# A first cross attention with scores by quarters of keys, transposed on VectorE, divided at the end on GpSimd

## The chip, the core and the metric

The kernel runs on one core of one Trainium2 chip. A core has a TensorE (matrix products, into the accumulator memory PSUM), a VectorE, a ScalarE (functions such as the exponential), a GpSimd and a SyncE that issues transfers; each works through its own queue in order, and they wait for each other through semaphores. PSUM has eight banks of 512 float32 words on each of 128 partitions. GpSimd does not appear in this kernel as a reader of PSUM. The metric is the device time of one execution in microseconds (us); less is better.

## The reference

The whole program is four layers of a perceiver, each a cross attention, a mixing block and a feed-forward block, with residual additions. The change is in the first cross attention alone. `x` is 16 batches of 64 query rows by 256, the context 16 batches of 1024 rows by 192; there are 16 heads of 16 columns:

```python
def _L0_xattn_ref(q_tokens, kv_tokens, Wq, Wk, Wv, Wo):
    q = q_tokens @ Wq.T
    k = kv_tokens @ Wk.T
    v = kv_tokens @ Wv.T
    ...
    attn = jnp.einsum('bhqd,bhkd->bhqk', q, k) * scale      # scale 1/4
    attn = jax.nn.softmax(attn, axis=-1)
    out = jnp.einsum('bhqk,bhkd->bhqd', attn, v)
    ...
    return out @ Wo.T

x = x + _L0_xattn_ref(_layernorm(x, axis=-1), ctx_768, ...)
```

## The kernel before, in words

`xattn_direct` (line 280) works batch by batch, and in each batch in four groups `c` of four heads, so in 64 steps `(b, c)`. Every operation on TensorE, VectorE (`dve`) and ScalarE (`act`) inside it goes through `in_order`, which ties each instruction to the one issued before it on the same engine: the order on these three engines is the order of the Python text. GpSimd's operations are not tied that way; the scheduler of the tile framework places them, in practice in the order of the text too.

A step of the loop at line 472 does work for three steps at once:

- `scores(*ahead)` (line 399): the scores of the next step, 4 heads by 64 queries by 1024 keys. The queries `qb` are stored so that a group of 32 partitions holds two heads, each multiplied by the mask of its own 16 rows (`own`), with zeros in the other's place. Two tiles `pss` of two banks each (e = 0, 1), 128 partitions (two heads by 64 queries) by 1024 keys, by four matmuls of 32 rows by 128 columns over 512 keys.
- `least` (line 408): VectorE's negated maximum of each tile. `exps` (line 413): ScalarE's exponential of a whole tile with that bias, and its sums by row. `shares` (line 419): VectorE's reciprocal of the sum and the multiplication of the exponentials.
- `transposes` (line 423): TensorE transposes of the exponentials in 128x128 blocks, 16 a step, into four PSUM banks in turn (`pst`), and a copy of each bank into `pT` by VectorE or ScalarE.
- `project` (line 356): a fourth of the key and value projections of the next batch (pieces 0, 1 keys; 2, 3 values), into two banks, copied out by VectorE and by ScalarE. Piece 0 issues the load of the next batch's transposed context on SyncE's queue.
- `values` (line 430): the products with the values for the step before, 32 matmuls of 128 rows by 32 columns over 64 queries, into a bank kept for all four groups (`both`). `keep` (line 442) copies it out once a batch.
- `queries(1, ...)` in steps 4 to 7 (second half of the query projections), `norm(1)` and `normed(1)` in steps 1 and 2, and `output` (line 447) once for two batches: product with `Wo` and the addition to `X`.

PSUM is divided into pools: `ps_s`, two tiles of two banks for the scores; `ps_t`, three banks for projections, transposes and the rest; `ps_o`, one bank for `both`. A tile of a pool is handed out in turn, and a writer waits until the readers of the tile's last use are done.

The second cross attention, `xattn_folded` (line 508), has forms that this change brings into the first one: scores by small column tiles, a stream transpose on VectorE, a matrix `same` that adds up quarters of the partitions. It is used below for durations.

Of the kernel before, what the change touches and what calls it, by code (L numbers as in the profile page):

```python
# [8 lines left out]
F32 = mybir.dt.float32  # L9
# [46 lines left out]
def bc(ap, axis, n):  # L56

    ap = ap.unsqueeze(axis)
    shape = list(ap.shape)
    shape[axis] = n  # L60
    return ap.to_broadcast(shape)
# [17 lines left out]
class Net:  # L79
# [113 lines left out]
    def copy(self, i, out, in_):  # L193

        if i % 2 == 0:
            self.nc.vector.tensor_copy(out, in_)
        else:
            self.nc.scalar.copy(out, in_)
# [81 lines left out]
    def xattn_direct(self, L):  # L280
# [6 lines left out]


        nc, tc, a = self.nc, self.tc, self.a
        dve, act = self.queue("dve", nc.vector), self.queue("act", nc.scalar)  # L290
# [5 lines left out]
        with ExitStack() as es:  # L296
            one = es.enter_context(tc.tile_pool(name=f"{L}one", bufs=1))
            two = es.enter_context(tc.tile_pool(name=f"{L}two", bufs=2))
            thr = es.enter_context(tc.tile_pool(name=f"{L}thr", bufs=2))
            ps_s = es.enter_context(tc.tile_pool(name=f"{L}ps_s", bufs=2, space=PSUM))  # L300
            ps_t = es.enter_context(tc.tile_pool(name=f"{L}ps_t", bufs=3, space=PSUM))
            ps_o = es.enter_context(tc.tile_pool(name=f"{L}ps_o", bufs=1, space=PSUM))

# [3 lines left out]
            )  # L307
            nc.vector.tensor_scalar(own, own, 0.25, None, ALU.mult)
            vs = [one.tile([P, NKC, H, 32], F32, name=f"v{i}") for i in range(2)]
            nc.gpsimd.memset(vs[0][:, :, :, 16:], 0.0)  # L310
# [41 lines left out]

            ctxs, kTs, os_ = {}, {}, {}
            both = ps_o.tile([P, 2, 4, TQ], F32, name="o")

            def project(b, piece):
# [6 lines left out]
                if piece < 2:  # L363
# [6 lines left out]
                    for i in range(2):  # L370
                        ms = slice((2 * piece + i) * 64, (2 * piece + i) * 64 + 64)
                        for n in range(2):
                            u, rows = (n ^ i) * 64, slice(n * 64, (n + 1) * 64)
                            self.mm(ps[i][u : u + 64, :], wk[rows, 1, ms], c1[rows, :], False, True)
                    for i, copy in enumerate((dve.tensor_copy, act.copy)):
                        copy(kTs[b][:, 2 * piece + i, :], ps[i])
                else:
# [7 lines left out]
                    for i in range(2):  # L385
                        for n in range(2):
# [7 lines left out]
                            )  # L394
                    for n, copy in enumerate((dve.tensor_copy, act.copy)):
                        j = 4 * n + 2 * jh
                        copy(v[:, j : j + 2, :, :16], ps[n].rearrange("p (i h d) -> p i h d", i=2, d=16))

            def scores(b, c):
                pss = [ps_s.tile([P, S], F32, tag="s", name="pss") for _ in range(2)]  # L400
                for n in range(2):
                    for e in range(2):
                        r = (n ^ (c % 2)) * 64 + e * 32
                        ql = qb[r : r + 32, c, b].rearrange("p h q -> p (h q)")
                        self.mm(pss[e][:, n * 512 : (n + 1) * 512], ql, kTs[b][r : r + 32, c, :])
                return pss

            def least(ps):
                nm = self.small.tile([P, 1], F32, tag="nm", name="nm", bufs=4)
                dve.tensor_reduce(nm, ps, AX.X, ALU.max, negate=True)  # L410
                return nm

            def exps(ps, nm):
                pr = thr.tile([P, S], F32, tag="pr", name="pr", bufs=4)
                sm = self.small.tile([P, 1], F32, tag="sm", name="sm", bufs=4)
                act.activation(pr, ps, AF.Exp, bias=nm, accum_out=sm)
                return pr, sm

            def shares(pr, sm):
                dve.reciprocal(sm, sm)  # L420
                dve.tensor_scalar(pr, pr, sm, None, ALU.mult)

            def transposes(dst, pr, jh, copy):
                pt = ps_t.tile([P, 512], F32, tag="t", name="pst")
                for j in range(4):
                    jj = jh * 4 + j
                    self.tr(pt[:, j * P : (j + 1) * P], pr[:, jj * P : (jj + 1) * P])
                copy(dst[:, jh * 4 : jh * 4 + 4, :], pt.rearrange("p (j q) -> p j q", q=P))

            def values(b, c, pT):  # L430
                o = both[:, b % 2]
                for j in range(NKC):
                    for h in range(4):
                        self.mm(
                            o[32 * h : 32 * h + 32, c, :],
                            vs[b % 2][:, j, 4 * c + h, :],
                            pT[:, j, h // 2, (h % 2) * TQ : (h % 2 + 1) * TQ],
                            j == 0,
                            j == NKC - 1,
                        )  # L440

            def keep(b):
                if b % 2 == 0:
                    os_[b // 2] = two.tile([P, 4, 2, TQ], F32, tag="oT", name="oT")
                act.copy(os_[b // 2][:, :, b % 2, :], both[:, b % 2])

# [12 lines left out]
            normed(0)  # L459
            project(0, 0)  # L460
            project(0, 1)
            for c in range(4):
                queries(0, c)
            steps = [(b, c) for b in range(B) for c in range(4)]
            pss = scores(0, 0)
            prs = [exps(pss[e], least(pss[e])) for e in range(2)]
            project(0, 2)
            project(0, 3)
            for p in prs:
                shares(*p)  # L470
            last = None
            for i, (b, c) in enumerate(steps):
                ahead = steps[i + 1] if i + 1 < len(steps) else None
                nxt, nms = [None, None], [None, None]
                if ahead:
                    pss = scores(*ahead)
                    nms = [least(ps) for ps in pss]
                pT = thr.tile([P, NKC, 2, P], F32, tag="pT", name="pT")
                transposes(pT[:, :, 0, :], prs[0][0], 0, act.copy)
                transposes(pT[:, :, 0, :], prs[0][0], 1, dve.tensor_copy)  # L480
                if ahead:
                    nxt = [exps(pss[e], nms[e]) for e in range(2)]
                    shares(*nxt[0])
                if b + 1 < B:
                    project(b + 1, c)
                if last:
                    values(*last)
                if ahead:
                    shares(*nxt[1])
                transposes(pT[:, :, 1, :], prs[1][0], 0, dve.tensor_copy)  # L490
                transposes(pT[:, :, 1, :], prs[1][0], 1, act.copy)
                if i == 1:
                    norm(1)
                if i == 2:
                    normed(1)
                if 4 <= i < 8:
                    queries(1, i - 4)
                if c == 0 and last:
                    keep(b - 1)
                if c == 1 and b % 2 == 0 and b > 0:  # L500
                    output(b // 2 - 1)
                prs, last = nxt, (b, c, pT)
            values(*last)
            keep(B - 1)
            output(NT - 1)
# [2172 lines left out]
```

## Time and profile before

| | us |
|---|---|
| median of three runs | 3171.4 (3170.1 to 3172.4) |
| the profiled execution | 3170.8 |
| its span, first to last instruction | 3168.8 |
| the stage of the change: first scores, and its last output product | 30.9 and 505.2 |

Mean granted TensorE clock of the profiled execution: 0.953; in the stage, from 58 to 500 us, it is 1.00. The engines' busy time in that stretch, whose length is 442.0 us:

| TensorE | VectorE | ScalarE | GpSimd |
|---|---|---|---|
| 436.2 | 371.8 | 251.8 | 9.1 |

A row of a group or of a timeline gives a line of the source (L72, L188, L191 are helpers through which all recorded operations pass), the engine (PE TensorE's matmuls, PEld its weight loads, DVE VectorE, ACT ScalarE, POOL GpSimd), the operation, the tiles it writes and reads (`out<-in`), its shape and a count. In a timeline the first two numbers are start and length; in brackets stands the idle time ahead and who ended it. A float32 matmul runs as two passes, so it counts twice. Matmuls of different row or column groups of the array overlap, so that the length of a group is not the sum of its parts. In the chain of waits, each piece starts where the one before it released it.

### The profile page before, as it was taken

How to read it: one execution, taken by the hardware profiler on the slowest of the kernel's cores; microseconds unless marked ns; L12 is line 12 of the kernel's file. 1: busy time of each engine (PE TensorE's matmuls, PEld its weight loads, DVE VectorE, ACT ScalarE, POOL GpSimd, SP SyncE). 2: the span in 40 equal slices, each digit the busy share in tenths (PEclk: the TensorE clock that was granted, in tenths of full speed). 3: DMA queues.
4: the chain of work that ended last, by engine and by line, in shares of the span. 5: the costliest groups of instructions: out<-in, count | busy, mean ns of one | idle time of the engine just before them, and what ended most of it. 6: DMA issues, size and time to landing. Idle time of an engine off the chain costs nothing.

```text
span 3168.8 us, 64106 instructions
## 1 busy us (share of the span) xinstructions
PE 2940.9 (93%) x26912; PEld 1772.9 (56%) x26912; DVE 1960.3 (62%) x4061; ACT 1348.4 (43%) x3035; POOL 712.7 (22%) x784
## 2 busy tenths in 40 slices
PE   7999999898899999979978999997999899998797
PEld 4666666665445544458854545434665455556676
DVE  6888886524666665971127676757884676765611
ACT  3555554312554541013324454438861255654211
POOL 1000002411110001014411000024771355541131
PEclk9999999999999999978988999998999999999889
DMA  2000000013223313017851222201111211210233
GB/s 74 32 32 32 28 22 15 14 37 105 61 78 92 98 45 82 21 65 270 294 162 53 70 71 73 59 21 39 41 54 37 64 57 63 70 44 14 94 108 122
DMA packets 73793, 223.00 MB, mean 70 GB/s; under 512 B 17457, under 2 KB 28580, under 8 KB 66594
## 3 DMA queue, kind: packets, MB, share of 16 engines
q1 hardware_dynamic: 45936, 113.99, 11.9%
q0 software_dynamic: 21840, 99.39, 9.4%
q10 hardware_dynamic: 5730, 5.53, 0.6%
q8 instruction: 212, 3.47, 0.5%
q14 instruction: 75, 0.61, 0.1%
HBM read 210.00 MB, written 12.66 MB: 70 GB/s over the span
## 4 chain that ended last, share of the span: by engine, by line
PE 79%; DVE 9%; issue 4%; ACT 4%; POOL 3%; DMA 1%; SPq 0%; ACTq 0%; POOLq 0%; DVEq 0%
PE pss L188 13%; PE o L188 12%; PE pu L188 6%; PE psp L188 5%; PE pkv L188 5%; PE pd L188 5%; PE py L188 4%; PE pst L191 4%; PE psc L188 3%; PE po L188 2%; DVE nm L72 2%; ACT pr L72 2%; PE pb L191 2%; PE psi L188 1%; PE psq L188 1%
## 5 line engine op out<-in xcount | busy, mean ns | idle before, releaser
L188 PE MATMUL pss<-cT,qw 128*32 128x256 f32 x8192 | 371.5, 387 | 23.0 <-ACT pr L72 23.0
L72 DVE TENSOR_REDUCE nm<-pss 128x2 f32<-128x512 f32 (+1 forms) x384 | 309.3, 861 | 86.3 <-PE pss L188 86.3
L188 PE MATMUL o<-pT,cx 128*64 128x512 f32 (+1 forms) x1024 | 355.4, 607 | 0.0
L72 ACT ACTIVATE pr<-pss,nmm 128x256 f32<-128x256 f32 x512 | 234.3, 483 | 164.8 <-DVE nmm L72 164.8
L188 PEld LDWEIGHTS pss<-cT,qw 128*32 128x32 f32 x8192 | 205.0, 110 | 173.0 <-ACT pr L72 33.1
L188 PEld LDWEIGHTS o<-pT,cx 128*64 128x64 f32 (+1 forms) x1024 | 127.8, 165 | 200.2 <-issue 187.8
L205 POOL TENSOR_SCALAR rs<-mv 128x8 f32<-128x8 f32 (+3 forms) x52 | 10.0, 193 | 877.1 <-DVE mv L221 444.4
L188 PE MATMUL pkv<-wx,cT 128*128 128x512 f32 (+1 forms) x512 | 193.3, 632 | 0.6 <-issue 0.6
L72 ACT ACTIVATE pr<-pr,sm 128x256 f32<-128x256 f32 x256 | 109.1, 497 | 184.2 <-DVE sm L72 184.2
L72 DVE TENSOR_SCALAR pr<-pr,sm 128x256 f32<-128x256 f32 (+1 forms) x384 | 170.6, 486 | 6.6
L72 DVE TENSOR_TENSOR_SCAN h<-dA,pb 128x512 f32<-128x512 f32 x128 | 154.5, 1217 | 15.8 <-PE pb L191 9.4
L1444 POOL TENSOR_TENSOR h<-h,cb 128x1024 f32<-128x1024 f32 x64 | 151.4, 2368 | 53.3 <-DVE h L72 51.0
L2304 DVE TENSOR_SCALAR y<-pd,row 128x256 f32<-128x256 f32 x39 | 18.9, 484 | 225.1 <-PE pd L188 175.7
L72 DVE STREAM_TRANSPOSE pT<-pr 128x1024 f32<-128x1024 f32 x128 | 151.8, 1224 | 2.2
L188 PE MATMUL pd<-wd,hT 128*128 128x256 f32 x656 | 149.3, 382 | 3.0 <-DVE hT L2492 1.4
L72 ACT ACTIVATE pr<-pss,nm 128x1024 f32<-128x1024 f32 x128 | 142.5, 1113 | 11.4 <-DVE nm L72 8.8
L191 PE MATMUL pst<-ident,pr 128*128 128x128 f32 x1024 | 140.6, 280 | 5.8 <-DVE sm L72 1.9
L72 ACT COPY pT<-pst 128x512 f32<-128x512 f32 x128 | 74.9, 585 | 163.8 <-PE pst L191 163.8
L191 PEld LDWEIGHTS pst<-ident,pr 128*128 128x128 f32 x1024 | 109.4, 141 | 61.5 <-ACT pT L72 26.5
L188 PEld LDWEIGHTS pd<-wd,hT 128*128 128x128 f32 x656 | 123.1, 190 | 31.4 <-DVE hT L2492 6.2
L1618 POOL TENSOR_TENSOR rnk<-rnk,mhalf 128x8 f32<-128x8 f32 (+1 forms) x84 | 130.0, 1548 | 7.0
L188 PE MATMUL py<-h,ident 128*128 128x512 f32 x256 | 130.7, 596 | 0.0
(525 smaller groups left out, 5700.2 us busy)
## 6 DMA issues: line engine op xcount, KB each, us to landing
cT<-in_ctxT SPq DMA_DIRECT2D x32, 768.0 KB, 4.4
cx<-in_ctxP SPq DMA_DIRECT2D x32, 768.0 KB, 4.3
cT<-in_ctxT SPq DMA_DIRECT2D x32, 512.0 KB, 4.3
cT<-in_ctxT SPq DMA_DIRECT2D x64, 256.0 KB, 6.1
offb<-d_off SPq DMA_DIRECT2D x16, 576.0 KB, 3.6
cb<-d_C SPq DMA_DIRECT2D x16, 512.0 KB, 3.8
wu<-in_L_ffn_w POOLq DMA_DIRECT2D x8, 1024.0 KB
wd<-in_L_ffn_w POOLq DMA_DIRECT2D x8, 1024.0 KB
```

What stands on the lines that cost most here:

```text
L72: ins = getattr(self.engine, op)(*args, **kwargs)
L188: self.in_order(self.nc.tensor.matmul(out, lhsT=lhsT, rhs=rhs, start=start, stop=stop))
L191: self.in_order(self.nc.tensor.transpose(out, in_, self.ident))
L205: nc.gpsimd.tensor_scalar(t[:p, :n], in_, scale, eps, ALU.mult, ALU.add)
L1444: nc.gpsimd.tensor_tensor(hs[i], hs[i], cbs[hf, g], ALU.mult)
L1618: nc.gpsimd.tensor_tensor(r, r, self.mhalf[:, : n * H], ALU.pow)
L2304: nc.vector.tensor_scalar(y[:, i, :], po[:, i * D : (i + 1) * D], weight[:, g + i : g + i + 1], None, ALU.mult)
```

## The change

It rewrites the step of the first cross attention:

- **PSUM.** `ps_s` has three tiles of two banks instead of two; `ps_t` two banks instead of three; `ps_o` goes. The output `o` of each step takes a bank of `ps_t`.
- **Scores** by quarters. The 128 partitions of a tile hold, for a group of 32, a quarter `qa` of the keys (every fourth run of 32 keys); the columns hold the halves of the keys `n`, the four quarters `q` of the query rows (two heads by two halves of 32 queries), and 128 keys. 64 matmuls of 32 rows by 32 columns over 128 keys take the place of four.
- **Maximum.** `largest` reduces a tile to four columns; GpSimd copies the four groups of partitions to one (`nw`), VectorE takes their minimum of the negated values (`least`), and GpSimd copies it to the other groups of partitions.
- **Exponentials** in four instructions a tile, a column of bias and of sums each.
- **Transposes.** `turn` is one VectorE stream transpose (32x32 blocks) per tile, straight into `pT`.
- **Division.** The exponentials are no longer multiplied. Once a batch `sums` adds the four groups' sums on TensorE, `inverse` takes the reciprocal and GpSimd spreads it over a masked matrix `rd`, `spread` turns that into a multiplier for each output on TensorE, and `keep` copies outputs and multiplier out and multiplies them on GpSimd.
- **Order.** The step transposes the first tile, then takes the maxima and the first tile's exponentials of the next step, then projections, values and `keep`, then the second tile's transpose and exponentials. `output` runs in the third group of a batch instead of the second.

```diff
-            ps_s = es.enter_context(tc.tile_pool(name=f"{L}ps_s", bufs=2, space=PSUM))
-            ps_t = es.enter_context(tc.tile_pool(name=f"{L}ps_t", bufs=3, space=PSUM))
-            ps_o = es.enter_context(tc.tile_pool(name=f"{L}ps_o", bufs=1, space=PSUM))
+            ps_s = es.enter_context(tc.tile_pool(name=f"{L}ps_s", bufs=3, space=PSUM))
+            ps_t = es.enter_context(tc.tile_pool(name=f"{L}ps_t", bufs=2, space=PSUM))
...
+            same = one.tile([P, 32], F32, name="same")
+            nc.vector.tensor_reduce(same, self.ident.rearrange("p (a x) -> p x a", x=32), AX.X, ALU.add)
+            fourth = one.tile([P, 32], F32, name="fourth")
+            nc.vector.memset(fourth, 0.25)
...
             def scores(b, c):
-                pss = [ps_s.tile([P, S], F32, tag="s", name="pss") for _ in range(2)]
-                for n in range(2):
-                    for e in range(2):
-                        r = (n ^ (c % 2)) * 64 + e * 32
-                        ql = qb[r : r + 32, c, b].rearrange("p h q -> p (h q)")
-                        self.mm(pss[e][:, n * 512 : (n + 1) * 512], ql, kTs[b][r : r + 32, c, :])
+                pss = [ps_s.tile([P, 2, 4, P], F32, tag="s", name="pss") for _ in range(2)]
+                kT = kTs[b][:, c].rearrange("p (k a y) -> p k a y", a=4, y=32)
+                for q in range(4):
+                    for n in range(2):
+                        for e in range(2):
+                            r = (n ^ (c % 2)) * 64 + e * 32
+                            for qa in range(4):
+                                self.mm(
+                                    pss[e][qa * 32 : (qa + 1) * 32, n, q, :],
+                                    qb[r : r + 32, c, b, q // 2, q % 2 * 32 : q % 2 * 32 + 32],
+                                    kT[r : r + 32, :, qa, :],
+                                )
                 return pss
...
+            def largest(ps):
+                nm = self.small.tile([P, 4], F32, tag="nm", name="nm", bufs=4)
+                dve.tensor_reduce(nm, ps.rearrange("p n q k -> p q n k"), AX.XY, ALU.max, negate=True)
+                w = self.small.tile([32, 4, 4], F32, tag="nw", name="nw", bufs=4)
+                for qa in range(4):
+                    nc.gpsimd.tensor_copy(w[:, qa], nm[qa * 32 : (qa + 1) * 32])
+                return w
+            def least(w):
+                m = self.small.tile([P, 4], F32, tag="nmm", name="nmm", bufs=4)
+                dve.tensor_reduce(m[:32], w.rearrange("p a q -> p q a"), AX.X, ALU.min)
+                nc.gpsimd.tensor_copy(m[32:64], m[:32])
+                nc.gpsimd.tensor_copy(m[64:], m[:64])
+                return m
+            def exps(b, c, e, ps, m):
+                if (c, e) == (0, 0):
+                    sms[b] = two.tile([P, 4, 2, 4], F32, tag="sm", name="sm")
+                pr = thr.tile([P, 4, 2, P], F32, tag="pr", name="pr", bufs=3)
+                for q in range(4):
+                    act.activation(
+                        pr[:, q], ps[:, :, q, :], AF.Exp, bias=m[:, q : q + 1], accum_out=sms[b][:, c, e, q : q + 1]
+                    )
+                return pr
+            def turn(b, c, e, pr):
+                if e == 0:
+                    pTs[b, c] = thr.tile([P, NKC, 2, 4, 32], F32, tag="pT", name="pT")
+                dve.transpose(
+                    pTs[b, c][:, :, e].rearrange("p k q x -> p q k x"),
+                    pr.rearrange("p q n (k y) -> p q (n k) y", y=32),
+                )
...
+            def sums(b, o):
+                ps = o[:, TQ : TQ + 32]
+                for qa in range(4):
+                    self.mm(ps[qa * 32 : (qa + 1) * 32], same, sms[b].rearrange("p c e q -> p (c e q)"))
+                return ps
+            def inverse(b, ps):
+                rc = two.tile([P, 32], F32, tag="rc", name="rc")
+                dve.reciprocal(rc, ps)
+                rds[b] = two.tile([P, 4, 2, 2, 2 * 32], F32, tag="rd", name="rd", bufs=1)
+                for c in range(4):
+                    nc.gpsimd.tensor_tensor(
+                        rds[b][:, c].rearrange("p e h (u x) -> p (e h u) x", x=32),
+                        bc(rc[:, 8 * c : 8 * c + 8], 2, 32),
+                        bc(same, 1, 8),
+                        ALU.mult,
+                    )
+            def spread(b, o):
+                for h in range(4):
+                    self.mm(o[32 * h : 32 * h + 32, P : P + 256], fourth, rds[b][:, :, h // 2, h % 2, :])
+            def keep(b, c, o):
+                if c == 0:
+                    oss[b] = two.tile([P, 4, TQ], F32, tag="os", name="os", bufs=1)
+                act.copy(oss[b][:, c], o[:, 0:TQ])
+                if c == 3:
+                    ra = two.tile([P, 4, TQ], F32, tag="ra", name="ra", bufs=1)
+                    act.copy(ra, o[:, P : P + 256].rearrange("p (c q) -> p c q", q=TQ))
+                    if b % 2 == 0:
+                        os_[b // 2] = two.tile([P, 4, 2, TQ], F32, tag="oT", name="oT")
+                    nc.gpsimd.tensor_tensor(os_[b // 2][:, :, b % 2, :], oss[b], ra, ALU.mult)
...
             for i, (b, c) in enumerate(steps):
                 ahead = steps[i + 1] if i + 1 < len(steps) else None
+                now = prs
                 if ahead:
                     pss = scores(*ahead)
+                turn(b, c, 0, now[0])
+                if ahead:
+                    ws = [largest(ps) for ps in pss]
+                    prs = [exps(*ahead, 0, pss[0], least(ws[0])), None]
                 if b + 1 < B:
-                    project(b + 1, c)
+                    projected(b + 1, c)
+                if last or c == 3:
+                    o = ps_t.tile([P, 512], F32, tag="t", name="o")
+                if c == 3:
+                    total = sums(b, o)
                 if last:
-                    values(*last)
+                    if last[1] == 3:
+                        spread(last[0], o)
+                    values(*last, o)
+                    keep(*last, o)
+                turn(b, c, 1, now[1])
                 if ahead:
-                    shares(*nxt[1])
+                    prs[1] = exps(*ahead, 1, pss[1], least(ws[1]))
+                if c == 3:
+                    inverse(b, total)
...
-                if c == 1 and b % 2 == 0 and b > 0:
+                if c == 2 and b % 2 == 0 and b > 0:
                     output(b // 2 - 1)
...
+            o = ps_t.tile([P, 512], F32, tag="t", name="o")
+            spread(B - 1, o)
+            values(*last, o)
+            keep(*last, o)
             output(NT - 1)
```

`projected` is `project` followed by its two copies, VectorE's of the first bank and ScalarE's of the second, as before.

## The prediction

> **What bounds the kernel now.** I read the page's slices first, then the chain that ended last, cut to steps of the first cross attention (about 31 to 505 us), then the timeline of the same steps. The change touches nothing else, so everything after 505 us only shifts. The chain (start, length, what) through one step:
>
> ```profile
> 153.79 1.03 PE o L188 x64
> 154.82 1.02 PE pst L191 x8
> 155.84 1.07 PE pss L188 x8
> 156.91 1.02 PE pst L191 x8
> 157.94 2.79 PE psp L188 x16
> 160.73 1.03 PE o L188 x64
> ```
>
> Every piece begins where the last one ends and all are TensorE: the step is 6.94 us (7.03 where keys are projected, psp then 2.89), and TensorE is its bound. VectorE is the next: from the groups of this stretch, with count, busy time, mean ns, and idle time ahead:
>
> ```profile
> L72 DVE TENSOR_REDUCE nm<-pss 128x1 f32<-128x1024 f32 x128 | 150.7, 1219 | 40.1 <-PE pss L188 40.1
> L72 DVE TENSOR_SCALAR pr<-pr,sm 128x1024 f32<-128x1024 f32 x128 | 96.7, 756 | 4.6
> L72 DVE COPY pT<-pst 128x512 f32<-128x512 f32 x128 | 87.7, 685 | 5.1 <-PE pst L191 1.2
> ```
>
> Per step that is two of each, about 5.3 us, and 0.69 for its share of the projections. So removing TensorE work alone can bring little over a microsecond a step, before VectorE binds.
>
> **TensorE's share.** Both pst pieces go: -2.04 us a step. The scores become 64 matmuls of 32x32 tiles over 128 columns, two passes each: 128 instructions in 8 rounds of 16 tiles. pst shows 128 columns in about 0.109 us (8 in 1.02, the rest being the change of tile shape). Do 16 tiles run side by side? The rows say so for 4 (o: 64 passes of 64 columns in 1.03 us) and, in the second attention, for 8:
>
> ```profile
> 905.90 1.96 PE L188 MATMUL pss<-cT,qw 64*32 64x256 f32 x64
> ```
>
> 64 passes of 256 columns, at 0.216 each if alone, take 1.96 us, 8 at a time. For 16 I take 8 x 0.109 and 0.17 for the first load and the change of shape: 1.05, as much as the 4 matmuls cost now. The upper end is 16.1 ns an instruction, o's 1.03/64: 128 x 16.1 = 2.06 us. A rule speaks against the change: the Trainium skill, "TensorE: Matmul & The Clock Gate", section "Wait — 56ns, not 53.3ns?", says that starts never lie closer than about 25 ns, however small the matmul. That would make 3.2 us, and take back the transposes. The rows contradict it: o's 64 in 1.03 us are already closer on average, so I don't use it. New on TensorE too: per batch `sums` (8 passes of 32 columns, 0.15) and `spread` (8 of 256, four at a time, 0.55), 0.2 a step. Sum: psp 2.84 + o 1.03 + 1.05 + 0.2 = 5.1 us.
>
> **The other engines' totals.** VectorE loses shares (2 x 0.94) and pT copies (2 x 0.68); it gains two stream transposes (2.37 for a pair below) and two small reductions (0.17, as nmm's copies of 32x8 take 0.165): 2.36 + 2.37 + 0.34 + 0.69 = 5.8. ScalarE: 8 exponentials at 0.45, 0.59 for the projection, 0.24 for `keep`: about 4.6. GpSimd: 12 small copies, and per step one 128x256 product of `inverse`: about 2.8. By totals the step would be 5.8 us. But the order decides, and it closes a loop.
>
> **The loop.** Of three score tiles, each step takes two, so the second tile of step s+1 is the first of step s. TensorE may write it only when the exponentials of step s's first tile are done. In ScalarE's order those come first; then, in every engine's order: scores(s+1) on TensorE, largest of both tiles on VectorE (after turn of step s), 4 + 4 copies on GpSimd, least, 2 copies on GpSimd, exponentials of s+1. The first tile's two copies stand in GpSimd's queue behind the second tile's four, so both reductions lie on the path. Rows for it, exponentials and transposes of the second attention:
>
> ```profile
> 900.35 0.47 ACT L72 ACTIVATE pr<-pss,nmm 128x256 f32<-128x256 f32 x1 [1.87 <-DVE nmm L72]
> 900.72 0.19 ACT L72 ACTIVATION_READ_ACCUMULATOR pr<-pss,nmm 128x1 f32 x1
> 900.81 0.47 ACT L72 ACTIVATE pr<-pss,nmm 128x256 f32<-128x256 f32 x1
> 901.46 2.37 DVE L72 STREAM_TRANSPOSE pT<-pr 128x1024 f32<-128x1024 f32 x2
> ```
>
> One exponential every 0.45; the fourth ends with its readout: 3 x 0.45 + 0.57 = 1.93. That scores wait for the readout is shown at the stage's end:
>
> ```profile
> 493.04 1.11 ACT L72 ACTIVATE pr<-pss,nm 128x1024 f32<-128x1024 f32 x1
> 494.05 0.19 ACT L72 ACTIVATION_READ_ACCUMULATOR pr<-pss,nm 128x1 f32 x1
> 494.30 0.31 PEld L188 LDWEIGHTS pss<-kT,qb 32*128 32x128 f32 x6 [0.84 <-ACT pr L72]
> ```
>
> The readout ends at 494.24, weights load at 494.30: 0.06. Small GpSimd copies the trace shows only as these:
>
> ```profile
> 504.86 0.23 POOL L789 COPY upto<-leq 64x64 f32<-64x64 f32 x1 [13.03 <-ACT pT L72]
> 505.04 0.23 POOL L790 COPY after<-gts 64x64 f32<-64x64 f32 x1
> 505.31 0.23 POOL L789 COPY upto<-leq 64x64 f32<-64x64 f32 x1
> 505.49 0.24 POOL L790 COPY after<-gts 64x64 f32<-64x64 f32 x1
> ```
>
> 64 elements: 0.23 long, 0.18 apart when independent; the dependent third starts 0.27 after. Fewer elements cost less (the 64x256 copies take 0.40, so 0.9 ns each): 4 elements would be 0.125 apart. Small tensor_scalars of 4 elements take 0.19. I take 0.15 apart and 0.185 long; ends 0.03 (one-element memsets of 0.1) and 0.25 (no overlap). Hand-overs: VectorE to GpSimd 0.08, GpSimd to ScalarE 0.05.
>
> Loop: 0.06 + scores 1.16 (1.05 and the last matmul's latency) + 0.05 + reductions 2.36 + 0.08 + four copies and the next start 0.60 + copy 0.185 + 0.08 + copy 0.185 + 0.05 + 1.93 = **6.75 us**, turn's 1.2 lying beside the scores. Against 6.98 a step the gain is 0.23, not 1.2: all four engines have slack, and what was hidden (the maximum's trip, the exponentials) binds. `inverse`'s four products (0.67 apart, from the 0.72 of 128x256 rows) run beside turn and largest, so cost nothing up to 0.9 each; at 1.3 they delay the copies and cost some 28 us in all.
>
> Costed at nothing: `keep` on ScalarE every step (0.24, ra 0.38 once a batch), hidden by about 2 us of slack there, at its own length otherwise; `same` and `fourth` at the start (about 0.3), beside the root of the first norm on GpSimd; the context's loads on SP, one per batch, 4.4 us to landing, unmoved. The weight loads that GpSimd issues for the next stage (0.8 each, three) now stand among the copies: 2 us at most, half of it slack, left out.
>
> **Extras now in the loop.** Transposes, projections and outputs share two banks instead of three, so psq and psy take the bank of psp's second half, whose ScalarE copy is queued behind the exponentials; and the next turn is queued on VectorE behind their result.
>
> ```profile
> 505.18 1.99 PE L188 MATMUL psy<-wo,oT 128*128 128x256 f32 x8 [0.47 <-ACT oT L72]
> 507.21 0.42 DVE L72 TENSOR_TENSOR X<-X,psy 128x256 f32<-128x256 f32 x1 [3.65 <-PE psy L188]
> ```
>
> psy: 0.65 until the bank is free, 2.03, 0.42, turn 1.2, statistics 0.6, instead of 1.27: +3.6 (now 1.74). psq: 0.65 + 1.95 + 0.75 + 1.2 - 1.27: +3.3 (now 1.75). The next weights' scaling, which nothing waits for now, stands on GpSimd in front of the copies of the last batch's second step:
>
> ```profile
> 487.35 4.49 POOL L794 TENSOR_SCALAR wo<-wo,pcol 128x256 f32<-128x256 f32 x4 [4.07 <-DMA wo<-in_L_attn_out_proj_wT]
> ```
>
> 4.5, of which 0.9 is slack: +3.6.
>
> **Sum**, from the first scores (30.9) to the last psy. Before: 505.2 - 30.9 = 474.3. After: to the second scores 11.6 (scores 1.2, reductions 2.4, copies 1.15, exponentials of both tiles 3.7, ScalarE's copy 0.6, which now frees the bank for the second value projection, 2.6); 62 x 6.75 = 418.5; the last loop and tail 16.3 (6.75, exponentials 2.0, turn 1.25, reciprocal 0.25, four products 2.8, spread and values 1.7, copies 0.65, product 0.85); psq 4 x 3.3 = 13.2; psy 7 x 3.6 = 25.2; the other half's norm 3.8; the next layernorm's roots and products, also on VectorE between turn and largest, 5; wo 3.6. Total 497.2: **+22.9**. The last four steps, which project nothing and take 5.3 now, are in it at 6.75. The profiled execution is 3170.8 (span 3168.8 and 2.0 around it), 0.6 below the median of 3171.4: 3168.8 + 22.9 + 2.0 = **3194**.
>
> **Rivals.** *Totals decide* (5.8 a step): 1.2 x 56 = 67 less, some 3110; for it, VectorE's idle time is small even now; against, the loop follows from the orders. 4%. *The same loop with cheap copies*, the case on the other side: at the memsets' pace, 0.03 apart and 0.1 long, the loop is 6.2, held at 6.4 where `inverse` interferes, and the sum -9: 3161. Each 0.01 us of a copy is worth 3.8 us; the sign turns at about 0.09 apart. Against it: no copy or tensor_scalar here is that short. 11%. *Scores bound by issue*, 2.06: the loop grows by 1.0, +53 on top: 3246. 10%. *GpSimd at 0.25 apart, or slow broadcast products*: about +28 on top, 3221. 15%. *That the third tile hides nothing* is no rival but the forecast's core.
>
> **Chances.** The loop at 6.5 to 7.1 has 60%, own range 3174 to 3212. Changes under 0.2% (6 us) can't be told from none. Faster: the first two rivals, 15%. Same: 8%, the loop's lower end (6.5). Slower: 77%. The range leaves out the totals' case and the worst scores: 3164 to 3236.
>
> **Right or wrong.** In the profile after: 128 pss instructions in about 1.05 us a step, no pst; TensorE idle over a microsecond a step, released by ScalarE's pr; a chain alternating pss, nm, the small copies, pr. Copies of nw 0.15 apart. If the chain shows VectorE alone, or nm starts with no wait for pss, the loop is wrong; if psy costs under 2 us, the bank's wait is.

## The result, and the profile after

| | us, median | lowest to highest | ratio to before, same session |
|---|---|---|---|
| before | 3171.9 | 3170.1 to 3189.2 | |
| changed | 3321.1 | 3313.3 to 3332.6 | 1.046 (1.041 to 1.051) |

The change is slower by 149 us, where 22.9 had been worked out and 3236 was the upper end. From the first scores to the start of the last addition to X (the eighth `X<-X,psy`) the stage takes 476.3 us in the profile before and 627.7 after: 151 more. What follows it takes 2662 and 2665. So the whole difference lies in this stage, and the stage's length is used below beside the times: the rest of the kernel, which no experiment touches but for one line in the last, varied from 2658 to 2692 us among the profiled executions, more than some of the effects sought.

Two lines of the page, the granted clock in 40 slices and the queue that carries instructions:

```profile
PEclk9988898799999999997898999998998999999879
q8 instruction: 267, 4.37, 0.5%
```

Before, that queue had 212 packets (3.47 MB), and every slice of the stage showed 9. Now five of the first eight show 7 or 8: the stage has 25 stretches of half clock, 157 us, where it had none. The chain of waits through one step and the start of the next shows four things at once:

```profile
196.59 5.18 PE psp L188 x16
...
204.17 1.67 PE pss L188 x89
205.84 1.12 issue
206.96 0.48 PE pss L188 x19
...
207.47 2.37 DVE nm L72 x2
...
209.88 0.18 POOL nw L433
...
210.10 0.18 POOL nw L433
...
210.32 0.18 POOL nw L433
...
210.53 0.18 POOL nw L433
...
210.77 0.19 POOL nmm L440
...
211.01 0.19 POOL nmm L441
...
211.22 1.05 ACT pr L72 x5
...
212.49 0.67 ACT pr L72 x3
...
213.21 1.84 PE pss L188 x97
215.05 3.04 PE psp L188 x16
```

The forecast's circle is there: scores, largest, the small copies, exponentials, scores. The copies stand 0.22 us apart, not 0.15. The scores run 1.84 us before projections can start where all is well (the second block; its first matmuls stand before the piece). In the first block TensorE stops for 1.12 us in the middle, with nothing it waits for on record ("issue"). And the projection at 196.59 takes 5.18 us, the one at 215.05 3.04: half clock against full. The groups of the stage after (30 to 650 us), busy time, mean ns, and idle time ahead:

```profile
L188 PE MATMUL pss<-kT,qb 32*32 32x128 f32 x8192 | 152.7, 304 | 62.7 <-issue 40.8 <-ACT pr L72 21.5
L433 POOL COPY nw<-nm 32x4 f32<-32x4 f32 x512 | 90.6, 177 | 271.4 <-DVE nm L72 254.8 <-DVE nmm L72 0.9
L72 DVE TENSOR_REDUCE nm<-pss 128x4 f32<-128x1024 f32 x128 | 150.4, 1217 | 75.4 <-PE pss L188 75.4
L188 PE MATMUL psp<-cT,wk 128*64 128x512 f32 x240 | 85.7, 854 | 0.0
```

40.8 us of TensorE's idle time ahead of pss are such stops, inside blocks of scores. The same 240 matmuls of psp took 58.1 us before. Summed over all projections of the stage, the pieces take 222.7 us instead of 183.4, with 22 of 62 over 3.6 us: some 39 us for the clock, in this one kind of work.

**What the stops are.** Of the 27 gaps of over 1 us between two score matmuls, 25 end 1.22 to 1.59 us after a 16 KB packet on the instruction queue has finished. All 24 gaps that the trace puts down to "issue" are among them; the other three stand under ScalarE's `pr`. Packets come every 5.9 us on average, so ends within 0.37 us of each other are no chance. Three of them, with times from the trace in us:

```
gap in pss        packet on q8      packet's end to gap's end
192.61-195.12     192.73-193.66     1.46
205.57-206.96     204.37-205.64     1.32
233.69-235.38     233.06-233.93     1.45
```

Each score matmul comes with a load of its weights, so one step's 128 matmuls are 256 instructions. Their size follows from the second experiment below, which has 15,360 instructions and 60 packets more than the kernel before: 60 x 16,384 bytes over 15,360 is 64 bytes each. So one step's scores are just one packet; TensorE goes through it in 1.7 us, and the packet alone takes 0.9 to 1.3. The queue is idle most of the time all the same: the stage's 107 packets take 110 of its 628 us. What sets the start of a packet, no run shows.

### The profile page after: what moved, and what is told of

Read it like the earlier page. It is cut to its first block, busy times and chain, and to the rows that moved or that the text cites. A ratio compares the mean times of both kernels' runs of the same rounds, so it can differ in the third digit from the quotient of the medians.

```text
span 3323.0 us, 79776 instructions
## 1 busy us (share of the span) xinstructions
PE 2954.4 (89%) x33824; PEld 1774.7 (53%) x33824; DVE 1937.3 (58%) x3951; ACT 1369.1 (41%) x3739; POOL 897.2 (27%) x1632
## 4 chain that ended last, share of the span: by engine, by line
PE 72%; DVE 11%; issue 6%; ACT 6%; POOL 4%; DMA 1%; SPq 0%; ACTq 0%; POOLq 0%; DVEq 0%
PE pss L188 14%; PE o L188 10%; PE pu L188 6%; PE pkv L188 5%; PE pd L188 5%; PE psp L188 4%; ACT pr L72 4%; PE py L188 4%; DVE nm L72 3%; PE psc L188 3%; PE po L188 2%; PE pb L191 2%; PE psi L188 1%; PE psy L188 1%; PE psq L188 1%
## 5 line engine op out<-in xcount | busy, mean ns | idle before, releaser
L72 ACT ACTIVATE pr<-pss,nmm 128x256 f32<-128x256 f32 x1024 | 471.8, 486 | 467.3 <-POOL nmm L441 249.4
L72 DVE STREAM_TRANSPOSE pT<-pr 128x1024 f32<-128x1024 f32 x256 | 309.4, 1228 | 30.0 <-ACT pr L72 20.7
L188 PE MATMUL pss<-kT,qb 32*32 32x128 f32 (+2 forms) x8576 | 192.2, 313 | 63.0 <-issue 40.8
L72 ACT ACTIVATION_READ_ACCUMULATOR pr<-pss,nmm 128x1 f32 x1024 | 223.2, 218 | 0.0
L188 PEld LDWEIGHTS pss<-kT,qb 32*32 32x32 f32 (+1 forms) x8576 | 117.1, 110 | 117.2 <-issue 70.3
L433 POOL COPY nw<-nm 32x4 f32<-32x4 f32 x512 | 90.6, 177 | 271.4 <-DVE nm L72 254.8
L188 PE MATMUL psp<-cT,wk 64*64 64x512 f32 (+1 forms) x512 | 126.0, 755 | 0.8 <-DVE kT L72 0.8
```

The lines of the kernel that those rows point to most:

```text
L72: ins = getattr(self.engine, op)(*args, **kwargs)
L188: self.in_order(self.nc.tensor.matmul(out, lhsT=lhsT, rhs=rhs, start=start, stop=stop))
L433: nc.gpsimd.tensor_copy(w[:, qa], nm[qa * 32 : (qa + 1) * 32])
```

## The experiments

The theory after this reading, A in the expectations: the *number* of TensorE instructions costs three times, in the loop, in stops for fetching, and in the half clock behind the stops; the forecast's loop, with its copies sized again, is the rest. B differs from run to run. Stage lengths are from one profiled execution each.

| kernel | score instructions a step | us, median | ratio (95%) | stage, us | half clock in it, us |
|---|---|---|---|---|---|
| before | 8 | | | 476.3 | 0 |
| changed | 128 | 3321.1 | 1.046 (1.041 to 1.051) | 627.7 | 157 |
| 1 few | 8 | 3230.2 | 1.016 (1.011 to 1.020) | 539.7 | 89 |
| 2 before, small | 128 | 3258.4 | 1.024 (1.020 to 1.029) | 562.8 | 27 |
| 3 order | 128 | 3325.1 | 1.045 (1.040 to 1.050) | 628.0 | 147 |
| 4 half | 64 | 3250.8 | 1.022 (1.018 to 1.027) | 561.3 | 85 |
| 5 order held | 128 | 3287.2 | 1.040 (1.035 to 1.044) | 591.4 | 96 |
| 6 half, order held | 64 | 3218.0 | 1.017 (1.013 to 1.021) | 516.6 | 58 |
| 7 other order | 64 | 3212.0 | 1.012 (1.008 to 1.016) | 505.6 | 71 |
| 8 the same, small | 128 | 3222.4 | 1.018 (1.015 to 1.021) | 529.8 | 75 |
| 9 other order, mended | 64 | 3190.0 | 1.001 (0.999 to 1.003) | 472.3 | 39 |
| 10 mended again | 64 | 3159.2 | 0.994 (0.992 to 0.997) | 468.8 | 51 |

### 1. The changed kernel with four large score matmuls

```diff
-                for q in range(4):
...
+                for n in range(2):
+                    for e in range(2):
+                        r = (n ^ (c % 2)) * 64 + e * 32
+                        ql = qb[r : r + 32, c, b].rearrange("p h q -> p (h q)")
+                        self.mm(pss[e][:, n].rearrange("p q k -> p (q k)"), ql, kTs[b][r : r + 32, c, :])
```

> The changed kernel with its scores computed by 4 matmuls of 32x128 tiles over 512 columns (8 instructions a step instead of 128); queries and keys then stand in other places of the score tiles, so the stage's output is another one, and the kernel is read for its time alone. Theory A (the number of TensorE instructions costs three times: 16.6 ns each in the loop, stalls in which instructions are fetched, and the half clock that follows the long stalls): scores 1.05 us instead of 1.95, the loop 7.7 -> 6.85, 62 x 0.85 = 53 us; the 41 us of stalls inside the scores go; the clock stays at 1.0 in the stage, some 25 us: about 3200 us. Theory B (the half clock comes from TensorE's waits for the other engines, and the gaps are waits that the records do not show): only the 53 us go, about 3268 us, and the clock is still halved in 15 or more windows of the stage, since TensorE waits even longer.

The stage loses 88 us, between the two. The stops are gone, as A had it:

```profile
L188 PE MATMUL pss<-kT,qb 32*128 32x512 f32 x512 | 127.2, 702 | 12.2 <-ACT pr L72 12.0
L188 PE MATMUL o<-pT,v 128*32 128x64 f32 x4096 | 75.4, 228 | 25.0 <-DVE v L72 13.0 <-DVE kT L72 12.0
```

No "issue" is left in the first row. But the clock is still halved for 89 us, as B had it: TensorE waits 12 us for exponentials and 25 for the bank that VectorE's copies free (second row), and these waits do it too. So 88 of the 151 us hang on the number of instructions, and 68 of the 157 us of half clock; the other 89 belong to the stage's order.

### 2. The kernel before with small score matmuls

```diff
-                        self.mm(pss[e][:, n * 512 : (n + 1) * 512], ql, kTs[b][r : r + 32, c, :])
+                            for qa in range(4):
+                                self.mm(
+                                    pss[e][qa * 32 : (qa + 1) * 32, n * 512 + k * 128 : n * 512 + (k + 1) * 128],
+                                    qb[r : r + 32, c, b, qa // 2, qa % 2 * 32 : qa % 2 * 32 + 32],
+                                    kTs[b][r : r + 32, c, k * 128 : (k + 1) * 128],
+                                )
```

(inside a further loop over four quarters k of the columns)

> The kernel before with only its scores by 64 matmuls of 32x32 tiles over 128 columns (128 instructions a step instead of 8), everything else as it was. Theory A: TensorE is the bound there, so every step grows by 0.6 to 0.9 us (2 us instead of 1.07), 64 x 0.75 = 48, and stalls inside the scores add 20 to 50: 3240 to 3270 us; more instruction fetches than the 212 packets before. Theory B, also the forecast's view of the scores (16 tiles side by side, 1.05 us): within 10 us of 3172.

A, in the middle of its range: the stage grows by 86 us, with the transposes, the tiles and every other order as before, and the instruction queue has 272 packets instead of 212. The lower quartile of its steps is 7.70 us, instead of 6.94, and the stops show in one row (two more, of 1.72 and 2.14 us, stand ahead of `pst`):

```profile
L188 PE MATMUL pss<-kT,qb 32*32 32x128 f32 x8116 | 128.9, 279 | 19.7 <-issue 19.2
```

The clock is halved in six short stretches in the stage. Each begins 2 to 4 us after the start of a stop of 2.19 to 3.13 us; the two ahead of `pst` brought none. This also shows that the kernel before is bound by TensorE, as the forecast read it: what is added there comes out at the end.

### 3 and 5. GpSimd's copies in another order

```diff
-                    ws = [largest(ps) for ps in pss]
-                    prs = [exps(*ahead, 0, pss[0], least(ws[0])), None]
+                    nms = [largest(ps) for ps in pss]
+                    prs = [exps(*ahead, 0, pss[0], least(gathered(nms[0]))), None]
+                    w1 = gathered(nms[1])
```

`largest` now ends with the reduction, and `gathered` makes the four copies.

> The changed kernel with one order changed on GpSimd: the two copies that spread the first tile's largest come before the four copies of the second tile instead of behind them. Theory A's loop: the four copies (0.87 us) leave the loop, 62 x 0.87 = 54 us, less what the next bound takes back (TensorE's pieces sum to about 6.1, VectorE's to 5.8, so nothing): about 3267 us, 3255 to 3285. Theory B (the loop is not what sets the step; the stalls and TensorE's own total do): under 15 us gained.

3325 us, no gain, but also no test: the order of the program's text isn't that of GpSimd's queue, though the description of the kernel before takes it so "in practice". In the trace the second tile's four copies still stand ahead of the first tile's two, as a scheduler had put them. The run shows how far the changed kernel repeats itself: 628.0 us for the stage against 627.7. For the fifth run the copies were also tied to each other, one after the other (`gps.tensor_copy` through the queue helper that VectorE and ScalarE already use).

> The edit of the third experiment once more, now with the order of GpSimd's copies held by dependencies (in the third the copies' places in GpSimd's queue had stayed as they were, so it showed only how well the changed kernel repeats itself). Theory A (the loop sets the step, stalls come on top): 0.87 us less a step, 3321 - 62 x 0.87 = about 3267. Theory B (a block of 256 TensorE instructions has to be fetched in each step, and the fetch sets the pace wherever it is late): the wait only moves from the copies to the fetch, less than 20 us gained.

36 us less in the stage, between the two: part of the loop's gain was eaten by stops, which rose from 40.8 to 56.2 us:

```profile
L188 PE MATMUL pss<-kT,qb 32*32 32x128 f32 x8105 | 139.1, 291 | 67.7 <-issue 56.2 <-ACT pr L72 11.4
```

TensorE waits 10 us less for exponentials and 15 longer for instructions: where it arrives earlier, the packet hasn't.

### 4 and 6. Half as many score instructions

```diff
-                            r = (n ^ (c % 2)) * 64 + e * 32
+                        r = (c % 2) * 64 + e * 32
...
-                                    pss[e][qa * 32 : (qa + 1) * 32, n, q, :],
+                                pss[e][qa * 32 : (qa + 1) * 32, q],
                                     qb[r : r + 32, c, b, q // 2, q % 2 * 32 : q % 2 * 32 + 32],
-                                    kT[r : r + 32, :, qa, :],
+                                kT[r : r + 32, :, qa, :],
```

The projection puts both halves of a head pair's keys side by side in one row group (`kTs` is 128 x 2 x 1024), so `kT` has 256 columns here, and 32 matmuls do what 64 did.

> The changed kernel with the keys of a head pair kept in one row group, so that its scores take 32 matmuls of 32x32 tiles over 256 columns (64 instructions a step instead of 128) at the same number of column passes, 8 tiles side by side: about 8 x 0.216 + 0.17 = 1.9 us, as much as the 128 take now. Theory A: the loop stays at 7.7, the stalls (41 us) fall to a half or less, and with them the windows of half clock: about 3285 us, 3270 to 3300. Theory B (stalls do not depend on the number of instructions): 3321 within 10.

More than A had: 66 us less in the stage. As many column passes, half as many instructions, and the stops nearly vanish:

```profile
L188 PE MATMUL pss<-kT,qb 32*32 32x256 f32 x4096 | 164.4, 404 | 14.0 <-ACT pr L72 9.7 <-issue 3.4
```

With 8, 64 and 128 score instructions a step (runs 1, 4 and the changed kernel) the stops are 0, 3.4 and 40.8 us: not in proportion. In this order 64 fit beside the rest, 128 don't.

> The fourth experiment's kernel (scores by 32 matmuls over 256 columns) with the same held order of GpSimd's copies. Stalls are nearly gone there (3.4 us), so the loop is seen bare. Theory A: its undisturbed step goes from about 7.2 to 6.35 (TensorE's own pieces sum to 6.2 to 6.3 there), 3251 - 50 = about 3200. Theory B: something else than the loop sets 7.2 (for one, TensorE's wait for the bank that VectorE's copy of the projection frees): less than 15 us gained.

The same order held on this kernel, where hardly any stop is left: 45 us less, 0.7 us a step over all. A batch without psq or psy goes from 7.44 to 6.96 us a step, and 27 us of half clock go too. That is the forecast's loop seen bare: what shortens GpSimd's queue shortens the step. It falls short of A's 6.35 and 50; TensorE's wait for the projection's bank (24 us ahead of `o`, as in the first run) is still there, and is the likely reason, though no run took it away by itself.

### 7 and 8. An order in which no loop closes within a step

```diff
                 if b + 1 < B:
-                    projected(b + 1, c)
+                    copies = project(b + 1, c)
+                    dve.tensor_copy(*copies[0])
+                if ahead:
+                    pss = scores(*ahead)
+                if last:
+                    turn(*last, 1, old)
...
+                turn(b, c, 0, now[0])
...
+                    prs = [exps(*ahead, 0, pss[0], m), exps(*ahead, 1, pss[1], least(w1))]
```

The sixth kernel's parts, in another order; the scores are issued tile by tile.

> The stage in another order, with scores by 32 matmuls over 256 columns: a score tile holds one half of the queries for both halves of the keys, the scores of a step's first tile are all issued before the second's, the projection stands ahead of the scores, turn of the second tile comes one step later, the exponentials of both tiles come at the end of a step. A tile's trip from scores to the end of its exponentials (about 6.2 us) then spans three tiles, a step and a half, instead of closing in one step. Theory A: no loop is left, TensorE is busy nearly all the time at full clock, the step is its pieces' sum of 6.3 us: stage about 440 us instead of 476 before and 628 after the change, 3130 to 3165 us in all. Theory B (the two banks for everything but scores set the pace): as slow as the sixth, about 3200 or more.

The undisturbed steps take 6.0 to 6.3 us, which is A's figure and the sum of TensorE's pieces (here 6.08 from one psp to the next; chain of waits: one behind the other, all TensorE):

```profile
398.23 3.06 PE psp L188 x16
401.29 1.89 PE pss L188 x64
403.17 1.14 PE o L188 x64
404.31 3.04 PE psp L188 x16
```

But the total missed: one or two steps in every four take 8.2 to 8.4, and those with a psq 11.3 to 12.7. In the chain these are a reciprocal behind which the projection's bank stays taken, and GpSimd's output product ahead of two small copies:

```profile
394.52 0.74 POOL oT L512
...
395.31 0.19 POOL nmm L72
...
395.55 0.19 POOL nmm L72
395.77 1.93 ACT pr L72 x8
397.70 0.48 ACT kT L72
...
413.06 0.35 DVE rc L72
413.41 0.04 issue
413.45 2.17 PE psp L188 x12
```

So one of the two causes is B's, a wait for one of the two banks. Runs 9 and 10, which keep the two banks and change the order, take most of it away.

> The seventh kernel's order with the change's own 128 score instructions a step (tile by tile: 64 matmuls of 32x32 tiles over 128 columns). Column passes and everything else as in the seventh, so the difference is the number of instructions alone. Theory A: fetch stalls of 20 to 45 us and some windows of half clock after them: the seventh plus 25 to 70 us. Theory B (the instructions' number hurts only where the loop is tight): within 10 us of the seventh.

24 us more in the stage than the seventh, just under A's 25, from one execution each; 10 in the medians, which is still B's (their ranges overlap by a little: 3194 to 3219 and 3217 to 3234). The time doesn't decide, but the trace shows A's stops. They have moved. No pss row shows them; the next block does:

```profile
L188 PE MATMUL o<-pT,v 128*32 128x64 f32 x4096 | 82.0, 229 | 30.6 <-issue 25.5 <-DVE pT L72 4.9 <-DVE v L72 0.2
```

### 9 and 10. The late pieces put elsewhere

```diff
                 if c == 3:
                     total = sums(b, o)
+                    rc = inverse(b, total)
+                if 4 <= i < 8:
+                    queries(1, i - 4)
+                if c == 2 and b % 2 == 0 and b > 0:
+                    output(b // 2 - 1)
                 if ahead:
                     prs = [exps(*ahead, 0, pss[0], m), exps(*ahead, 1, pss[1], least(w1))]
+                if ra is not None:
+                    divided(last[0], ra)
+                if c == 3:
+                    products(b, rc)
```

> The seventh kernel with what its trace showed to be late put elsewhere: the reciprocal of the sums stands ahead of the second tile's small reduction on VectorE, GpSimd's products behind the last small copies of a step, the second half's query projections and the outputs ahead of the exponentials, and in the first step the projection behind the scores. In the seventh's trace the undisturbed step is 6.24 us, but two steps in every batch of four take 8.2 to 8.4, and those with query projections 12.3. Theory A: those steps come down to about 6.5 (30 us), 7 and 8.5 (15 us), the clock stays full in the middle of the stage: stage 450 us instead of 505 (before: 476), 3145 us, 3135 to 3160, faster than both kernels. Theory B (the two banks that projections, values, outputs and queries share hold up every step that needs a third): 3190 or more.

33 us less in the stage than the seventh, which brings it to 472, against 476 before; the ratio of 1.001 can't be told from none. Query steps came down to 8.9 to 9.2, about as expected; the steps with the reciprocal stayed at 7.7, since it still stood behind a transpose on VectorE:

```profile
407.19 2.07 DVE nm L72 x2
409.26 0.09 issue
409.35 0.15 DVE nmm L72
409.50 1.15 DVE pT L72
410.65 0.26 DVE rc L72
410.90 0.04 issue
410.95 2.10 PE psp L188 x12
```

> The ninth kernel with two more places moved: the reciprocal of the sums right behind the two large reductions on VectorE (in the ninth's trace the step with it takes 7.7 us instead of 6.1, since the projection waits for the sums' bank), and the next stage's scaling of its output weights behind this stage's last products on GpSimd (there it holds up the small copies from 459 to 468 us). Theory A: 14 x 1.5 + 8, about 29 us less in the stage: 443 us instead of 472, against 476 before, so 30 us faster than before in the same runs, ratio 0.990. Theory B (the bound is already TensorE's total): under 8 us gained, no difference from before that can be told.

Run 10 moves the first tile's `least`, the gathers and the first `turn` behind `inverse`, and ties the scaling of the next stage's weights to the last of `products`.

A ratio of 0.994 (0.992 to 0.997): faster than both kernels, by 0.6% and not by A's 1%, and not B's "no difference" either. Where the 0.6% arises isn't shown. In the profiled executions the stage is only 3.5 us shorter than the ninth's, within B, and 7.5 shorter than before; the profiled execution of run 10 took 3172.0 us, 13 above its median. In it the step with the reciprocal is 6.5, but the next one 6.95 instead of 6.24 (`spread` waits 9 us in all for GpSimd's products), and the last steps, without projections, run 34 us at half clock. Up to there the clock holds, but for 17 us in the first steps (columns: us of the stretch, busy time of PE, PEld, DVE, ACT, POOL with counts, granted clock, DMA share, GB/s):

```profile
30.00:455.00 425.00, 399.54 (x8855) 233.82 (x8852) 341.87 (x472) 271.70 (x1085) 174.22 (x791) 0.98 0.10 32
```

TensorE is busy for 94% of it, at 0.98. In the changed kernel it was 76% and 0.88 for 30 to 650.

## Why the prediction was wrong

**The sign and the loop held.** The kernel before is bound by TensorE (run 2). Behind the change the step is set by the order: three score tiles with two taken per step tie a step's scores to the last step's exponentials, and the small copies lie on that path (the chain, and runs 5 and 6). An undisturbed step, of which there are eight, shows it bare:

```profile
340.02 1.84 PE L188 MATMUL pss<-kT,qb 32*32 32x128 f32 x120 [0.49 <-ACT pr L72]
341.83 2.36 DVE L72 TENSOR_REDUCE nm<-pss 128x4 f32<-128x1024 f32 x2 [0.58 <-PE pss L188]
344.24 0.83 POOL L433 COPY nw<-nm 32x4 f32<-32x4 f32 x4 [0.30 <-DVE nm L72]
345.37 0.18 POOL L441 COPY nmm<-nmm 64x4 f32<-64x4 f32 x1
345.59 0.47 ACT L72 ACTIVATE pr<-pss,nmm 128x256 f32<-128x256 f32 x1 [3.20 <-DVE v L72]
```

The last row names VectorE's copy of `v` as what released ScalarE, but by the program the exponential doesn't read it. It happens to end at 345.57 us, 0.02 after the copy at 345.37, which the exponential does need. From the end of one step's first exponentials to the next's this step takes 7.55 us: 0.05 until TensorE writes again, 1.57 from there to the start of the last matmul, 0.24 until VectorE reads, 2.36 for the reductions, 1.40 to the exponentials' start, 1.93 for them. The forecast had 6.75; of the 0.80 between, two terms make all.

**Wrong first: the scores at 1.05 us.** The step that failed is "For 16 I take 8 x 0.109 and 0.17 for the first load and the change of shape: 1.05". Four and eight tiles side by side were shown; sixteen were inferred. Measured: 1.64 to 1.72 us from the first start to the last in blocks without a stop, 13 ns an instruction. In the loop the first 8 go ahead into the third tile, and 1.57 + 0.24 = 1.81 stand where the forecast had 1.16 + 0.05: 0.60 a step more, over half of the way to the rival "scores bound by issue", which added 1.0 and had one chance in ten. The rule on starts not under 25 ns (the Trainium skill, "TensorE: Matmul & The Clock Gate", "Wait — 56ns, not 53.3ns?") was rightly not taken for its figure, since 13 is measured; but that the rows contradict the figure was no reason to drop what it says in kind, a least time from start to start however small the matmul. The row that contradicted it, o's 16.1 ns an instruction, would have been the nearer price.

**Wrong second: the copies of GpSimd at 0.15.** They are 0.18 long and 0.22 apart, 0.24 for the second of a dependent pair. From the end of the reductions to the exponentials that makes 1.40 us where the forecast's terms make 1.18: 0.22 a step more. Both together are the 0.80; 62 x 0.80 = 50 us.

**Too large: psq and psy, and luck in a total.** A step with a psq takes 9.99 us, and 6.75 + 3.3 had been worked out. That agrees by luck: on a loop of 7.55 the extra is 2.4, not 3.3. With a psy it is 10.3 in steps without a stop, an extra of 2.7 and not 3.6. Together they are 10 us less than forecast.

**Left out: the fetch.** No term and no rival held a cost for TensorE's instructions arriving late; it was put at nothing without a reason, and the stops are 40.8 us. The profile before had the queue's 212 packets in it, and the change's count of instructions was in the forecast; the two weren't put together.

**Left out: the clock.** The granted clock was full in the stage before, and was taken to stay so, though the forecast itself left TensorE idle over a microsecond in each step. About 39 us on the projections.

The sum closes. For the forecast's own span, to the start of the last psy, the change is 150 us (474.3 to 623.9), of which 23 were forecast. In it 62 steps take 590.8 us by the trace, where the forecast had 469.3 (418.5 for the loop, 51 for psq, psy, the norms and wo). Of the 121.5 between, 50 are the loop; 58 are scores that took longer than 1.57 us, from stops and half clock; 23 are scores that started late, all but 2 of them behind 3.4 us or more of half clock; psq and psy take off 10; the rest is 1. Another 5 lie before and behind these steps. Two of the rivals' totals were small by the forecast's own rates: scores at 2.06 would add 62 x 1.01 = 63 and not 53, copies 0.25 apart 38 and not 28. Neither alone reaches what was measured. Of the two terms left out, the runs show the fetch by itself (1, 2 and 4). The clock was not varied alone; its size is read from equal work at two speeds, and how much of the 81 us of longer and later scores is its own stays open.

## What to carry to other kernels

Count instructions beside columns: a matmul split sixteen ways has the same columns on paper, but here it cost 0.6 us a step in the loop, and it made TensorE's code too long to be fetched in time. Half as many with twice the columns (run 4) took back 66 of 151 us with the same result. Where a buffer closes a loop over several engines, cost each hop, then see whether another order lets the trip span more tiles (runs 7 to 10): that removed the loop (7.55 us a step to 6.0 to 6.3). And a scheduler's queue is read from the trace, not from the program's text (run 3).

## What was not expected of the hardware

- **TensorE stops for instructions within a block.** Packets of 16 KB take 0.9 to 1.3 us, and TensorE goes on 1.2 to 1.6 us after one ends. Stops are 1.1 to 3.9 us from start to start.
- **The clock falls with half idleness.** The Trainium skill, "TensorE: Matmul & The Clock Gate", Part 1, has the clock fall after an idle window of about 3.4 us, and rise after a busy one. The records here do change in steps of 3.4 us. But in run 1, 14 of the 15 falls follow a window in which TensorE was busy for 6 to 48% (one 67%), so a wait of some two microseconds in it is enough, as in run 2. In the changed kernel falls follow windows of 10 to 76%: all 12 windows at full clock in which it was busy for less than half, and 13 of the other 127. The rise is stricter: all 24 in the changed kernel's stage follow a window that was busy throughout, and half clock stayed after windows of 78 to 92% (and after one busy throughout); in run 7 some rises follow 90 to 97%. A step with a microsecond's idle time therefore keeps a half clock that one stop has brought. Here the measurement decides over "idle".
- **Many small matmuls start close together at first.** The first 32 of a block that starts undisturbed begin 6.7 ns apart, in two groups of 16; after a pause of some 0.2 us the later ones start 2 to 18 ns apart, 13 on average.
